# An MLP layer between scan layers: as a stage of its own, or in pieces beside the scan layers

## The chip, the cores and the metric

The kernel runs on one core of a Trainium2 chip, in one launch. The metric is device time in microseconds, the median of several executions. The core has five engines with a queue each: TensorE (PE), VectorE (DVE), ScalarE (ACT), GpSimd (POOL) and the sync engine (SP), which here only issues transfers. Each engine works through its own queue in order and waits on semaphores for the others.

## The reference

Eight images of 48 x 48 x 96, float32, go through four layers. Each layer is `x = x + layer(group_norm(x))`.

```python
x = x + _L0_conv_ref(_gn(x), ...)   # selective scan over the image in four directions
x = x + _L1_conv_ref(_gn(x), W1, b1, W2, b2, coef)
x = x + _L2_conv_ref(_gn(x), ...)   # four scans over rows and columns, restarted in each line
x = x + _L3_conv_ref(_gn(x), ...)   # as layer 0

def _L1_conv_ref(x, W1, b1, W2, b2, coef):
    xu = _upsample_rfft(xc)                          # to twice the size, band-limited
    h = h @ W1.T + b1                                # 96 -> 384
    h = coef[:, 0] + coef[:, 1] * h + coef[:, 2] * (h * h)
    h = h @ W2.T + b2                                # 384 -> 96
    out = _lpf_rfft(hc, cutoff=0.5)[:, :, ::2, ::2]  # low-pass, every second sample
```

Layers 0 and 3 are written once (`ss2d`), with their own weights. The images do not depend on each other.

## The kernel before

The four layers follow each other as four stages: `ss2d("l0")`, `spectral`, `lines`, `ss2d("l3")` (L1082 to L1085). Each opens its own pools of on-chip memory and closes them at its end, and hands its result on through HBM, one tensor an image (x1, x2, x3, L109).

**The scan layers.** `scans` (L188) lays out one long sequence by hand, and the order in which it calls engines is the order on their queues. There are 8 jobs (images) of 4 directions of 5 blocks of 10 or 8 rows: 160 blocks. A block has 8 slots (NG) in 4 turns, two slots a turn, a slot being some 4 us. In a turn ScalarE makes the decay factors `da` (L292, PSUM, two buffers) and copies a broadcast row `bc` to PSUM (`copy_b`, L249); VectorE and GpSimd share the inputs `dbu` (L268, four tiles, `rooms`); VectorE scans (L300); GpSimd multiplies by the output weights (`make_hc`, L306); TensorE sums over the states (`reduce`, L326 and L328), always for the turn before. The sync queue loads `bc` (L233) and `dd` (L221), which are sent to all partitions from a small copy in HBM that an earlier step stored (L446, L668).

**Work given out in slots.** At the end of each slot `aside(at)` (L370) issues what goes on the side: loads of the next block, one step of the generator `beside`, one step of stage 1 of a block two ahead (`run`), and the matmuls put in `tail`. In `ss2d` the generator `side` (L605) yields once per slot: the output work of the image before (`post`, L544), the group norm of the next image (`front`, L509), and its convolution (`conv`, L513). PSUM has eight banks: `da` takes four, `b` and `y` one each, and the two left are `s1` and `side` in `ss2d`, and `s1` with two buffers in `lines`.

**The MLP layer.** `spectral` (L893) uses that band-limiting is linear: the two image directions are enlarged and reduced by products with fixed matrices `upt` (48 x 73) and `downt` (73 x 48), and the square alone stays between. For each image: `heighten` (L921) enlarges one direction, and the result goes to HBM and back in another order; for 11 bands of 7 rows `widen` (L984) enlarges the other, `hidden` (L992) makes the 384 squares, `narrow` (L1001) brings them back to 96, `slim` (L1018) reduces one direction, and the result goes through HBM (`ydd`); `lower` (L959) reduces the other and adds the linear part, a product of x with a 96 x 96 matrix `wl` made from the norm (L951), the bias and x itself (L978, VectorE). `heighten` and `norm` of the next image and `lower` of the one before run beside the bands. Copies out of PSUM are shared between ScalarE and VectorE.

`lines` (L715) begins when `spectral` has closed its pools. Its `side` (L878) loads the next image after 8 slots and makes its norm later in the job.

Of the kernel before, what the change touches and what calls it, by code (L numbers as in the profile page):

```python
# [17 lines left out]
DH = 96  # L18
# [18 lines left out]
UR = 7  # L37
UCUT = (slice(0, 64), slice(64, UG))
NM = 3
# [58 lines left out]
def vss_stack_kernel(ctx: ExitStack, tc: tile.TileContext, i: dict, out: bass.AP):  # L98
# [41 lines left out]
    def group_norm(x, into, psum, behind=lambda step: step()):  # L140


        got = {}
        yield from norm_scale(x, got, psum, behind)
        for r0, nr in BLKS:
            nc.scalar.activation(into(r0, nr), x[:, r0:r0 + nr, :], AF.Identity, bias=got["shift"], scale=got["rs"])
            yield

    def norm_scale(x, got, psum, behind=lambda step: step()):
# [9 lines left out]
        for n in range(6):  # L159
            nc.vector.bn_stats(st[:, n, :], x[:, 8 * n:8 * n + 8, :])  # L160
            if n % 2:
                yield
        mv = small.tile([C, 2], F32, tag="mv", name="mv")
        nc.vector.bn_aggr(mv, st)
        yield
# [8 lines left out]
        for _ in range(7):  # L174
            yield
# [4 lines left out]
        yield  # L180
# [4 lines left out]
        yield  # L185


    def scans(dirs, order, restart, on_pool, a, pools, ps, stage1, opening, done, side, tail, ahead=None):  # L188
# [181 lines left out]
        def aside(at):  # L370

            nblk, slot = at // NG + 1, at % NG
            if nblk < len(blocks):
# [5 lines left out]
            next(beside, None)  # L379
# [3 lines left out]
            while tail:  # L383
                tail.pop(0)()

        for t, (b, q) in enumerate(turns):
# [29 lines left out]
            if q == NG // 2 - 1 and b.k == order[-1] and b.last:  # L416
                for _ in beside:
                    while tail:
                        tail.pop(0)()
        make_hc(nt - 1, 1)  # L420
# [50 lines left out]
    def ss2d(l, xin, xout, b0=0):  # L471
# [41 lines left out]
        def conv(b, blks, behind=lambda step: step()):  # L513
# [3 lines left out]
            for r0, nr in blks:  # L517
                n = nr * SEG
                for half in range(2):
                    pu = side_psum()  # L520
                    for slot in range(7):
                        for tap in ((0,), (1, 2), (3,), (4, 5), (6,), (7, 8), ())[slot]:
# [13 lines left out]
                        yield  # L536
# [4 lines left out]
                    yield  # L541
                    nc.sync.dma_start(zs[b][:, half, s], z[:, :n])

        def post(b, blks=BLKS):  # L544
# [4 lines left out]
            for r0, nr in blks:  # L549
# [8 lines left out]
                yield  # L558
                sq = lnp.tile([DH, 2, BMAX], F32, tag="sq", name="sq", bufs=1)
                nc.scalar.activation(sq[:, :, :n], yc, AF.Square)  # L560
                yield
# [7 lines left out]
                yield  # L569
            nc.scalar.activation(var[:, v0:v1], var[:, v0:v1], AF.Sqrt, bias=eps5[:CH])  # L570
            yield
            nc.vector.reciprocal(var[:, v0:v1], var[:, v0:v1])
            yield
            for r0, nr in blks:
                n = nr * SEG
                s = slice(r0 * W, r0 * W + n)
                z = lnp.tile([DH, LEAD + 2 * BMAX], F32, tag="zin", name="zin", bufs=1)
# [13 lines left out]
                yield  # L591
# [10 lines left out]
                yield  # L602
                nc.sync.dma_start(xout[b][:, s], xi[:, :n])

        def side(job):  # L605
# [9 lines left out]
            if job > 0:  # L615

                for _ in range(3):
                    used += 1
                    yield
                for _ in post(job - 1):  # L620
                    used += 1
                    yield
            if more:
                for _ in front(job + 1):
                    used += 1
                    yield

                while used < 10 * NG - 5:
                    used += 1
                    yield  # L630
                yield from conv(job + 1, BLKS, tail.append)
            else:

                for n, blk in enumerate(BLKS[:0:-1]):
                    while used < (NK * len(BLKS) - len(BLKS) + n + 1) * NG + 2:
                        used += 1
                        yield
                    for m, _ in enumerate(post(job, [blk])):
                        if m % 2:
                            used += 1  # L640
                            yield
# [61 lines left out]

        dirs, tail = DIRS_SS, []
# [4 lines left out]
        scans(dirs, (0, 1, 3, 2), False, ON_POOL_SS, a, pools, ps, stage1, opening, done, side, tail, conv(0, BLKS[1:3]))  # L709
        for _ in post(nb - 1, BLKS[:1]):  # L710
            pass
        stack.close()


    def lines(xin, xout):  # L715
# [8 lines left out]
        def load_x(b):  # L724
            xs[b] = xpool.tile([C, L], F32, tag="x", name="x")
# [16 lines left out]
        def front(b, behind=lambda step: step()):  # L742
            xp = xpads[b % 2]
            yield from group_norm(seq(xs[b], False), lambda r0, nr: shift(xp, 0, 0)[:C, r0:r0 + nr, :], lambda: ps("s1", 2),
# [22 lines left out]
        for k in range(NK):  # L767
            nc.vector.tensor_mul(taps[:, k], taps[:, k], wl["l2_inu"][:, k].unsqueeze(1).to_broadcast([DH, 4, 2 * DH]))
            for half in range(2):
                nc.scalar.activation(diag[:, k, half, :], wc["ident"], AF.Identity, scale=w["l2_d"][:, k, half:half + 1])  # L770

                p = ps("s1", 2)
# [3 lines left out]
        def stage1(b):  # L776
# [9 lines left out]
            def conv(half):  # L786
                def run():
                    got["u", half] = ps("s1", 2)
# [17 lines left out]
            def s3():  # L806
                got["p"] = ps("s1", 2)
# [8 lines left out]
            def s5():  # L816
                s4()
                for half in range(2):
                    got[half] = ps("s1", 2)
# [10 lines left out]
            def s7():  # L830
                for half in range(2):
                    got["z", half] = ps("s1", 2)
# [18 lines left out]
        def done(b, half, y):  # L851
# [8 lines left out]
            def project():  # L860
                got["o"] = ps("s1", 2)
# [16 lines left out]
        def side(job):  # L878
            if job + 1 < nb:
                for _ in range(NG):  # L880
                    yield
                load_x(job + 1)
# [6 lines left out]
        scans(dirs, range(NK), True, ON_POOL_L2, a, pools, ps, stage1, opening, done, side, tail)  # L889
# [3 lines left out]
    def spectral(xin, xout):  # L893
# [3 lines left out]
        stack = ExitStack()  # L897

        def pool(name, bufs, **kw):
            return stack.enter_context(tc.tile_pool(name=name, bufs=bufs, **kw))  # L900
        wt, xpool, xtp, xhp, upp, zp, row, pp, dr = (
# [277 lines left out]
```

## Time and profile before

| | us |
|---|---|
| median of 3 runs (18397.78 to 18404.0) | 18399.97 |
| span of the profiled execution | 18409.2 |
| first scan layer, from the first filling of its pipeline to its last VectorE work | 45 to 5585 |
| MLP layer, until the first memset of the lines layer | 5585 to 6913 |
| lines layer with its filling | 6913 to about 12650 |
| last scan layer | about 12650 to 18409 |

Busy over the whole span: TensorE 14747.1 us (80%), VectorE 16140.7 (88%), ScalarE 13666.8 (74%), GpSimd 15136.4 (82%). One 480-column float32 matmul is two records of the profile. A line of a waits view names who waited, for whom, and then the total in us, the number of times and the longest one. A line of a windows view gives a stretch of time, its length, the busy time and the number of instructions of each engine, the mean granted clock of TensorE as a share of full speed, the DMA engines' busy share, and GB/s.

### The profile page before, as it was taken

Reading aid. Unit: us, or ns where it says so; the run is one execution under the profiler, and the core shown is the slowest. Engines: PE = TensorE matmul, PEld = TensorE weight load, DVE = VectorE, ACT = ScalarE, POOL = GpSimd, SP = SyncE. Lnnn points to the kernel's source line nnn. Section 1 sums busy time; section 2 is a strip of 40 time slices with the busy share of each in tenths; the row PEclk is TensorE's granted clock in tenths of the full one; section 3 lists DMA queues with packets and bytes.
Section 4 is the critical chain, followed back from the end, with each engine's and each line's share of the span. In section 5 each row is a group of like instructions: output and inputs, shape, how many; then the busy total and the mean of one; then the engine's idle time right before and its main releaser. Section 6 shows DMA issues by size and latency. Waiting matters only on the chain.

```text
span 18409.2 us, 167554 instructions
## 1 busy us (share of the span) xinstructions
PE 14747.1 (80%) x53500; PEld 4297.8 (23%) x53500; DVE 16140.7 (88%) x10329; ACT 13666.8 (74%) x20348; POOL 15136.4 (82%) x7999
## 2 busy tenths in 40 slices
PE   7777777777777897888988988988777777777777
PEld 1211211211214562222222222222121221221221
DVE  7999999999992228999999999997899999999998
ACT  6877887887772227888788888886788778778776
POOL 7999999999990007888888888887899999999998
PEclk7877877777767787888888888888778778777776
DMA  4544545544443324444444444443454455455454
GB/s 143 175 171 171 172 172 172 174 174 167 172 168 52 50 43 148 158 150 152 156 149 156 150 155 156 148 155 125 164 178 171 169 173 173 170 175 173 166 174 144
DMA packets 768448, 2836.47 MB, mean 154 GB/s; under 512 B 235724, under 2 KB 298668, under 8 KB 640926
## 3 DMA queue, kind: packets, MB, share of 16 engines
q1 hardware_dynamic: 767558, 2825.75, 45.4%
q8 instruction: 418, 6.85, 0.2%
q14 instruction: 472, 3.87, 0.1%
HBM read 2377.32 MB, written 448.17 MB: 153 GB/s over the span
## 4 chain that ended last, share of the span: by engine, by line
POOL 27%; PE 20%; DVE 16%; issue 14%; ACT 14%; DMA 8%; SPq 1%; POOLq 0%; ACTq 0%; DVEq 0%
POOL dbu L306 18%; DVE dbu L300 10%; POOL dbu L268 6%; PE ps_s L792 5%; ACT ps_da L292 5%; DVE dbu L268 4%; DMA dd<-dds 3%; POOL dds L460 3%; PE ps_y L326 3%; ACT L292 2%; DMA dd<-dd 2%; PE ps_h L998 2%; PE ps_y L1011 2%; PE ps_s L864 1%; ACT L827 1%
## 5 line engine op out<-in xcount | busy, mean ns | idle before, releaser
L300 DVE TENSOR_TENSOR_SCAN dbu<-ps_da,dbu 128x968 f32<-128x968 f32 (+3 forms) x5760 | 11820.3, 2075 | 559.7 <-ACT ps_da L292 447.5
L306 POOL TENSOR_TENSOR dbu<-dbu,bc 128x1440 f32<-128x1440 f32 (+1 forms) x3840 | 10061.9, 2633 | 1615.3 <-DVE dbu L300 1540.9
L292 ACT ACTIVATE ps_da<-dd,w_l_a 128x484 f32<-128x484 f32 (+3 forms) x11520 | 7433.6, 649 | 2878.2 <-DVE dbu L300 2651.5
L326 PE MATMUL ps_y<-dbu,w_red 128*32 128x480 f32 (+1 forms) x23040 | 4838.4, 735 | 1955.6 <-POOL dbu L306 1935.4
L328 PE MATMUL ps_y<-dbu,w_red 128*32 128x480 f32 (+1 forms) x7680 | 4797.9, 735 | 0.0
L268 DVE TENSOR_TENSOR dbu<-dd,ps_b 128x962 f32<-128x962 f32 (+5 forms) x2880 | 3833.4, 1331 | 264.9 <-ACT ps_b L249 150.6
L268 POOL TENSOR_TENSOR dbu<-dd,bc 128x481 f32<-128x481 f32 (+5 forms) x2240 | 3910.5, 1760 | 22.6 <-DMA dd<-dd 19.5
L326 PEld LDWEIGHTS ps_y<-dbu,w_red 128*32 128x32 f32 x23040 | 748.5, 124 | 5975.6 <-POOL dbu L306 4242.9
L792 PE MATMUL ps_s<-xpad,w_l_cw 128*128 128x480 f32 (+1 forms) x2560 | 1758.5, 839 | 0.0
L249 ACT COPY ps_b<-bc 128x482 f32<-128x482 f32 (+3 forms) x2720 | 1450.5, 533 | 233.4 <-DVE dbu L268 191.4
L525 PE MATMUL ps_side<-xpad,w_l_cw 128*128 128x480 f32 (+1 forms) x2880 | 1526.5, 657 | 18.9 <-ACT u L538 14.2
L292 ACT ACT_TABLE_LOAD x986 | 1265.0, 1283 | 17.6
L734 POOL MEMSET xpad<- 128x2760 f32 x2 | 4.7, 2404 | 1333.9 <-DVE x L978 1333.9
L322 PE MATMUL ps_y<-ysum,w_ident 96*96 96x480 f32 (+1 forms) x960 | 762.9, 885 | 315.9 <-ACT ysum L701 315.3
L650 PE MATMUL ps_s<-bcl,dtw 6*96 6x480 f32 (+1 forms) x1280 | 871.7, 770 | 103.7 <-ACT dds L654 93.2
L660 PE MATMUL ps_s<-u,w_l_xp 96*38 96x480 f32 (+1 forms) x1280 | 832.3, 781 | 20.3 <-ACT z L540 20.3
L460 POOL TENSOR_TENSOR dds<-dds,u 96x960 f32<-96x960 f32 (+1 forms) x320 | 706.8, 2209 | 156.3 <-ACT dds L678 156.3
L525 PEld LDWEIGHTS ps_side<-xpad,w_l_cw 128*128 128x128 f32 x2880 | 559.8, 217 | 1032.4 <-issue 905.2
L792 PEld LDWEIGHTS ps_s<-xpad,w_l_cw 128*128 128x128 f32 x2560 | 521.2, 208 | 1084.6 <-issue 977.2
L328 PEld LDWEIGHTS ps_y<-dbu,w_red 128*32 128x32 f32 x7680 | 687.5, 124 | 0.0
L833 PE MATMUL ps_s<-xpad,w_l_inz 96*96 96x480 f32 (+1 forms) x640 | 506.3, 925 | 86.4 <-ACT dds L827 70.5
L654 ACT ACTIVATE dds<-ps_s,w_l_dtb 96x480 f32<-96x480 f32 (+1 forms) x640 | 404.7, 632 | 212.5 <-PE ps_s L650 94.7
(147 smaller groups left out, 11759.8 us busy)
## 6 DMA issues: line engine op xcount, KB each, us to landing
dd<-dd SPq DMA_DIRECT2D x512, 1452.0 KB
bc<-bcd SPq DMA_DIRECT2D x1536, 480.0 KB
dd<-dd SPq DMA_DIRECT2D x256, 1440.0 KB
dd<-dds SPq DMA_DIRECT2D x512, 363.0 KB
dd<-dd SPq DMA_DIRECT2D x128, 1164.0 KB
bc<-bcd SPq DMA_DIRECT2D x384, 384.0 KB
dd<-dds SPq DMA_DIRECT2D x256, 360.0 KB
dd<-dd SPq DMA_DIRECT2D x64, 1152.0 KB
```

Of the source, the lines that this page charges most:

```text
L249: nc.scalar.copy(bps[t][:, :bcs[t][0].shape[1]], bcs[t][0])
L268: engine.tensor_mul(o, du, by.unsqueeze(1).to_broadcast([P, hi - lo, by.shape[1]]))
L292: nc.scalar.activation(da[:, at:at + b.m], b.got[half][:, u % 3, 0, :], AF.Exp, scale=a[:, b.k, ci:ci + 1])
L300: nc.vector.tensor_tensor_scan(db, da, db, 0.0, ALU.mult, ALU.add)
L306: nc.gpsimd.tensor_mul(h, h, bcs.pop(2 * t + sub)[1].unsqueeze(1).to_broadcast([P, 3, n]))
L326: nc.tensor.matmul(y[32 * g:32 * g + 32, :n], lhsT=wc["red"][:, :32], rhs=hc[:, g, b.at], start=False, stop=(slot == 3))
L328: nc.tensor.matmul(y[DH:, :n], lhsT=wc["red"][:, 32:], rhs=hc[:, 2, b.at], start=(slot == 0), stop=(slot == 3))
L460: nc.gpsimd.tensor_mul(du, dt, u)
L525: nc.tensor.matmul(pu[:, :n], lhsT=flat[:, at:at + P], rhs=xpad[:, r0 + dy:r0 + dy + nr, dx:dx + W], start=(tap == 0), stop=(tap == 8))
L650: nc.tensor.matmul(got["p"][:DH, :n], lhsT=dtw[2 * NS:, b.k, half, :], rhs=b.bcl[2 * NS:, :n], start=True, stop=True)
L660: nc.tensor.matmul(got["p"][:NBC, :n], lhsT=w[f"{l}_xp"][:, b.k, half, :], rhs=u[:, half], start=(half == 0), stop=(half == 1))
L792: nc.tensor.matmul(got["u", half][:, :n], lhsT=flat[:, at:at + P], rhs=shifted(off), start=(tap == 0), stop=(tap == 3))
```

## The change

`spectral` is gone as a stage. A class `Guest` holds the MLP layer as a generator of small items, and `aside` gives them out at the end of each slot of the first scan layer and of the lines layer. An item is a transfer or a VectorE step ("do"), a pause of some slots ("wait"), or a piece with one PSUM bank ("psum"): its matmuls are issued in one slot and the copy out of PSUM, always on ScalarE, at the start of the next slot (`settle`). A credit limits the pieces: one a slot in the first scan layer, 0.42 in `lines`. Image b of the MLP layer can start when `post` has stored it (`avail`), and `lines` loads it when it is `made`.

The banks are those of the side work: in `ss2d`, `side` in slots in which the generator says that the bank is free (`yield True`), and `s1` in slots 2, 5 and 6; in `lines` the two buffers of `s1` become two named banks, `sa` and `sb`. So that `side` is free more often, `conv` issues its nine taps in slots 2 to 5 instead of 0 to 5.

The pieces are smaller: bands of 5 rows (15 an image), x transposed in four loads of 24 channels, the enlarged rows `xh` stored in four times two transfers in runs of 24 channels (96 bytes) instead of two of whole rows, `ydd` read back in 12 times two loads. x is loaded a second time for the last step. The residual is part of the matmul: the matrix is `wlin * rs + ident`, and the copy out of PSUM with the bias is the result. In `post`, `sq` and `zin` now share one buffer, and the descriptor memory for transfers (`dynamic_dma_scratch_size`) is set to 2048.

```diff
-UR = 7
+UR = 5
+HC = 24
+HS = 8
+ZW = 4
...
         def aside(at):
             nblk, slot = at // NG + 1, at % NG
+            if guest:
+                guest.settle()
...
-            next(beside, None)
+            clear = next(beside, True)
             run(at)
...
             while tail:
                 tail.pop(0)()
+            if guest:
+                guest.turn(slot, clear)
...
-                    pu = side_psum()
                     for slot in range(7):
-                        for tap in ((0,), (1, 2), (3,), (4, 5), (6,), (7, 8), ())[slot]:
+                        if slot == 2:
+                            pu = side_psum()
+                        for tap in ((), (), (0, 1), (2, 3), (4, 5), (6, 7, 8), ())[slot]:
...
-                        yield
+                        yield slot < 2
...
+            guest.banks = lambda slot, clear: (["side"] if clear else []) + (["s1"] if slot in (2, 5, 6) else [])
...
-                    got["u", half] = ps("s1", 2)
+                    got["u", half] = ps("sa" if half else "sb", 1)
...
-                got["o"] = ps("s1", 2)
+                got["o"] = ps("sa", 1)
...
+                while guest.made <= job + 1:
+                    for _ in range(NG):
+                        yield
                 load_x(job + 1)
...
+        guest.banks = lambda slot, clear: {0: ["sa"], 2: ["sb"], 3: ["sa"], 6: ["sb"]}.get(slot, [])
+        guest.rate = 0.42
...
+        def settle(self):
+            while self.pending:
+                self.pending.pop(0)()
+
+        def turn(self, slot, clear):
+            ready, self.soon = [f for n, f in self.soon if n <= 1], [(n - 1, f) for n, f in self.soon if n > 1]
+            for step in ready:
+                step()
+            self.credit = min(self.credit + self.rate, 2.0)
+            if self.wait:
+                self.wait -= 1
+                return
+            banks = self.banks(slot, clear)
+            while True:
+                self.item = self.item or next(self.work)
+                kind, *of = self.item
...
+                if kind == "do":
+                    self.item = None
+                    of[0]()
+                    continue
+                if not banks or self.credit < 1.0:
+                    return
+                self.item = None
+                self.credit -= 1.0
+                self.put(self.psum(banks.pop(0)), *of)
...
+                    nc.vector.scalar_tensor_tensor(wl, wlin, rs, wc["ident"], ALU.mult, ALU.add)
...
+                def load_xt(c0):
+                    nc.sync.dma_start(xt, self.xin[b].rearrange("c (h w) -> h c w", w=W)[:, c0:c0 + HC, :])
...
+                for c0 in range(0, C, HC):
+                    for s0 in range(0, HC, HS):
+                        yield heighten(s0)
+                    yield "wait", 1
+                    if c0 + HC < C:
+                        yield "do", lambda: load_xt(c0 + HC)
+                    yield "wait", 1
+
+                    def keep():
+                        for s in UCUT:
+                            nc.sync.dma_start(upd[s, :, c0:c0 + HC], xh[s])
+                    yield "do", keep
+                    yield "wait", 2
...
+                for n in range(last + 1):
+                    yield hidden(n, 0)
+                    if n:
+                        yield slim(n - 1)
+                    yield hidden(n, 1)
+                    yield hidden(n, 2)
+                    if n < last:
+                        yield widen(n + 1)
+                    yield narrow(n, 0, 3)
+                    if bands[n][1] > 3:
+                        yield narrow(n, 3, UR)
...
+                def lower(n):
+                    v = xv[:, n * ZW:(n + 1) * ZW, :]
+
+                    def run(p):
+                        nc.tensor.matmul(p[:C, :ZW * H], lhsT=wl, rhs=v, start=True, stop=False)
+                        for j in range(ZW):
+                            nc.tensor.matmul(p[:C, j * H:(j + 1) * H], lhsT=zs[n % 2][:, j, :], rhs=downt,
+                                             start=False, stop=(j == ZW - 1))
+                        self.soon.append((1, lambda: load_z(n + 2)))
+                    return "psum", run, lambda p: nc.scalar.activation(v, rows(p[:C], ZW * H), AF.Identity, bias=bl)
...
     ss2d("l0", i["x"], x1, guest)
-    spectral(x1, x2)
-    lines(x2, x3)
+    lines(x2, x3, guest)
     ss2d("l3", x3, out)
...
+                   dynamic_dma_scratch_size=2048)
```

The pieces of the other steps (`widen`, `hidden`, `narrow`, `slim`) have the matmuls of the old functions with the new band height.

## The prediction

> **What bounds the kernel now.** I read the busy shares over time first, then each stage's sums, then windows within one image's cycle of the first scan layer, then single waits and a few microseconds of single queues. Over time (a digit is a tenth of busy, a slice 460 us):
>
> ```profile
> DVE  7999999999992228999999999997899999999998
> ACT  6877887887772227888788888886788778778776
> POOL 7999999999990007888888888887899999999998
> ```
>
> Three slices near the first third have VectorE and ScalarE at 2 and GpSimd at 0: that is the MLP layer (L893 on), in which only TensorE works. By stage, from the windows view (first scan layer, MLP layer, lines layer):
>
> ```profile
> core 0: us, PE busy (x) PEld busy (x) DVE busy (x) ACT busy (x) POOL busy (x), PEclk, DMA share, GB/s
> 45.00:5584.95 5539.95, 4223.76 (x15382) 1084.33 (x15380) 5224.86 (x3183) 4316.33 (x6518) 5089.48 (x2856) 0.76 0.49 169
> 5584.95:6913.26 1328.31, 1154.55 (x6604) 757.32 (x6604) 274.10 (x465) 278.69 (x481) 0.00 (x0) 0.78 0.35 49
> 6913.26:12650.00 5736.74, 4953.88 (x15627) 1317.54 (x15628) 5255.66 (x3377) 4622.94 (x6637) 4793.94 (x2196) 0.83 0.42 153
> ```
>
> The scan layers are held by VectorE (94% and 92%), with GpSimd close in the first (92%). ScalarE has 1224 and 1114 us free there, TensorE 1316 and 783. The MLP layer needs 1155 us of TensorE, 553 of ScalarE and VectorE together. So the question is what ScalarE and TensorE can take without making VectorE wait. The first scan layer answers it by itself, since one image's cycle (680 us) has two halves: norm and output work of neighbours (first five windows) and then the convolution of the next image (L525), which loads both engines more. Two windows of each half:
>
> ```profile
> 836.00:904.00 68.00, 53.48 (x212) 17.94 (x204) 66.86 (x42) 50.78 (x78) 62.35 (x32) 0.68 0.47 162
> 1040.00:1108.00 68.00, 44.76 (x154) 7.43 (x146) 65.98 (x43) 50.83 (x77) 59.65 (x33) 0.58 0.40 140
> 1176.00:1244.00 68.00, 52.93 (x196) 13.13 (x188) 66.95 (x38) 59.27 (x87) 65.52 (x34) 0.94 0.51 175
> 1312.00:1380.00 68.00, 52.56 (x202) 13.92 (x200) 64.29 (x37) 57.99 (x88) 63.15 (x38) 0.87 0.56 194
> ```
>
> Columns as above. In the convolution half ScalarE has 58 to 59 us of 68 (85 to 87%) against 51 (75%), and yet each such window holds 25 scans where the other half holds 23 to 25. TensorE does some 50 more matmul records and is hardly busier, because the granted clock is 0.87 to 0.94 there against 0.58 to 0.68.
>
> Waits of VectorE in the whole first scan layer (us in total, times, longest):
>
> ```profile
> DVE dbu L300 <- ACT ps_da L292: 103.9, 135, 3.4
> DVE dbu L268 <- ACT ps_b L249: 74.5, 2, 73.9
> DVE xi L601 <- PE ps_side L598: 51.1, 19, 6.8
> ```
>
> The second is the filling of the pipeline; the first is what a busier ScalarE would raise: 0.77 us each time.
>
> **Removed.** From the last VectorE work of the first scan layer to GpSimd's first memset of the lines layer nothing but the MLP layer runs (POOL L734 waits 1333.9 us for DVE L978). 6913.26 - 5584.95 = **-1328.3**. The filling of the lines layer behind it (6913 to 6979) stays: its tiles take the memory of the closed layer, as before.
>
> **Added, VectorE.** Per image (rows of the first scan layer): 6 bn_stats by 0.536 = 3.2, aggregate 0.3, L171 1.37, L172 2.66, L173 0.16, L181 0.14, L183 0.37, and the new 96x96 scalar_tensor_tensor about 0.26 (as L1044): 8.3 us. By 8: **+66**, all on the bound. Every PSUM copy that VectorE made goes to ScalarE.
>
> **Added, ScalarE and TensorE.** In the built program's queues an image has 132 evacuations on ScalarE. By rows: xh 12 by 0.78 (L934's 0.97 for 480 columns, cut to 384), xu and hq 60 by 0.50 (L999, 0.688 for 511, cut to 365), ym 29 by 0.31 to 0.39 (L1014), yd 15 by 0.55, last step 12 by 0.45, plus two table loads of 1.28: 67 us. TensorE: 1154.55/8 = 144 us. The queue order puts 5.34 images beside the first scan layer (from its second image on) and 2.66 beside lines, the last stored after 543 of 640 loads of dd while lines fetches it at 564, so `while guest.made` never holds the lines layer up.
> First scan layer: 5.34 x 67 = 358 us of ScalarE over 132 blocks of 34 us, 6 to 8 items a block in the light half, 3 in the convolution half. The light half then stands at 75 + 10 = 85%, where the convolution half stands now without loss; the latter goes from 86 to 90%. I take one more 0.77 us wait in every second block: **+51**. Below it 0; above it all 358.
> Lines: 2.66 x 67 = 178 us over 112 blocks. Waits of VectorE on ScalarE are 281 by 0.82 us now; one more per two blocks is 46. TensorE, at 86%, gets 2.66 x 144 = 383 us over 112 x 35.9 = 4020, so 95%; VectorE waits 142 us on it now (L855, L872, L870), and half as much again over 112 of 160 blocks is 50. **+96**. Bounds 0 and 383 (TensorE wholly exposed). The two named banks, sa and sb, are part of this: a convolution or projection queued behind a guest evacuation waits for ScalarE, and behind it on TensorE stand the reductions, which have four dbu rooms (17 us) of cover.
> In a sentence beside this: the Trainium skill, "TensorE: Matmul & The Clock Gate", section "What's actually happening", has the gate open to full after about 3.4 us of sustained work. The windows above go that way, but twenty records of L930 back to back took 15.6 us at 0.50, so the trace agrees in part only; by the rule alone the 50 us would be nil.
>
> **Moved, the transfers.** All go through the one sync queue, in order, past dd (L221) and bc (L233). Per image 69 transfers instead of 19; at 0.4 us of issue that is 160 us more over 11 ms of a queue that mostly waits, nothing. The load_xt, up and z pieces are 240 to 1152 packets, 1 to 5 us. The store of xh is new in kind: it was 73 whole rows, it becomes 4 x 3504 runs of 96 bytes. The nearest row is the z load, 3504 runs of 384 bytes. In the timeline of the sync queue, start and length first:
>
> ```profile
> 6101.14 16.64 SPq L966 DMA_DIRECT2D z<-ydd  x2
> ```
>
> and in windows of 3 us under it, DMA share and GB/s at the end:
>
> ```profile
> 6106.00:6109.00 3.00, 0.00 (x0) 0.00 (x0) 0.00 (x0) 0.00 (x0) 0.00 (x0) 0.50 1.49 91
> 6109.00:6112.00 3.00, 0.00 (x0) 0.00 (x0) 0.00 (x0) 0.00 (x0) 0.00 (x0) 0.50 1.49 96
> ```
>
> At some 93 GB/s, 1314 KB take about 15 us, in which the queue itself stands. In the built order 10 of 24 such stores beside the first scan layer come right between the second dd load and the bc pair, 3 more just ahead of that dd load. How early is that pair? In the timelines of the sync queue and of ScalarE:
>
> ```profile
> 2030.38 6.94 SPq L233 DMA_DIRECT2D bc<-bcd  x2
> ```
>
> ```profile
> 2044.56 0.55 ACT L249 COPY ps_b<-bc 128x482 f32<-128x482 f32 x1
> ```
>
> 14 us ahead of its reader, of which its own way takes 3 or so. So 15 - 11 = 4 us late each time, and what is late is ScalarE's copy, with all da behind it and VectorE's scan behind these. I take it for each, since those elsewhere stand ahead of other dd or bc loads: 32 stores x 4 = **+128**; bounds 0 and 32 x 15 = 480. By the Trainium skill, "DMA: Bandwidth & Descriptors", section "Specifications", runs under 512 bytes are read-modify-written; it speaks against this edit, gives no price here, and no run shows it yet.
>
> **Costed at nothing.** Convolution taps bunched in slots 2 to 5 (both ss2d layers): same matmuls, covered by TensorE's idle fifth; uncovered, 2 us late at the reductions, which have 17. One buffer for sq and zin: the first zin load follows the last reader of sq by four steps; uncovered, the sync queue would stand a slot (4 us) once an image. The smaller descriptor scratch: every transfer of the page is issued on SPq.
>
> **Sum.** -1328.3 + 66 + 51 + 96 + 128 = -987. On the profiled execution's 18409.2: 17422. That execution is 9.2 above the median of the runs, 18399.97, so the forecast is **17,410**, with 17,280 to 17,600 as its own range.
>
> **Rivals.**
> (1) All hidden: the added matmuls raise the clock as in the convolution windows and ScalarE stays ahead. Only VectorE's 66 remain: 18400 - 1328 + 66 = 17,138. For it: no loss between the two halves. Against: the convolution half gets 3 items on top of its 86%.
> (2) The 96-byte stores stall at full price: 480 instead of 128: 17,765. For it: the queue standing 16.64 us; against: 14 us of lead and stores not always ahead of the pair.
> (3) ScalarE and TensorE exposed: 358 and 383 in place of 51 and 96: 18,007. For it: in-order queues, VectorE already waits on both in lines; against: the two halves.
> (4) Slower than before: every one of 1058 evacuations reaches ScalarE before its matmul is done, since it follows it by one slot only, and da waits behind. It decides from (1328 - 66)/1058 = 1.19 us each. The nearest row, L654, also one slot behind its matmul, waited for TensorE 38 times of 272, 0.92 us each; with that at every evacuation 0.51 + 0.92 = 1.43, by 1058 = 1513: 18,651. Against: 38 of 272.
> That the change doesn't do what it says would be a lines layer waiting for images; the order of the queues excludes it.
>
> **Chances.** The predicted time is the forecast's, the likeliest. Forecast 0.57, (1) 0.17, (2) 0.12, (3) 0.10, (4) 0.04. The range takes in (1) and (2), 17,130 to 17,800, and leaves (3) and (4) out. 0.2% (37 us) is about what a measurement tells from no change: faster 0.95, same 0.01, slower 0.04.
>
> **What would show it.** No stretch with GpSimd at 0 between the scan layers; the first scan layer's 5540 at 5600 to 5750 us, the 5737 of lines at 5800 to 5900, the last layer unchanged within 20; VectorE's waits on L292 up by 50 to 120; waits on DMA for bc or dd up by 100 or more, just behind stores of upd. It is wrong if the last layer changes, if waits on DMA do not rise, or if ScalarE's waits on TensorE exceed 300 us.

## The result and the profile after

| | before | after |
|---|---|---|
| median of the runs, us | 18401.99 (18397.78 to 18404.58) | 17895.1 (17876.22 to 17905.77) |
| span of the profiled execution | 18409.2 | 17891.2 |

The ratio is 0.9722, with a 95% interval of 0.9708 to 0.9736: faster by 2.8%. The forecast was 17,410, its range 17,130 to 17,800; the time lies above both. 1328 us were taken out and 518 came off the span.

In the busy view over 40 slices of the changed kernel, no slice has GpSimd at 0 any more:

```profile
DVE  7998999898888788787888889996999999999998
ACT  6877878878787677787777778786878778778776
POOL 7988888888888677787777778886999999999998
```

The ends of the stages are read from GpSimd's rows of the tile `xpad`, which give, behind the three durations in ns, the first and the last start of its two memsets. Lines begins at the first number of L755, the last layer at the last number of L490 (its second memset is that of the last layer):

```profile
L490 POOL MEMSET xpad<- x2: 2182/2184/2187, 0.9 to 12324.4; 128x2500 f32 x2
L755 POOL MEMSET xpad<- x2: 2403/2406/2409, 5996.0 to 5998.3; 128x2760 f32 x2
```

In the kernel before, the second memset of the last layer starts at 12,816.7, after the last work of lines (VectorE's last addition to x starts at 12,816.6). So lines ends there, 167 us later than the "about 12650" from which the 5737 us of lines was taken; only the boundary moves. Read so in every run (the first layer before is 6913.3 less the MLP layer's 1328):

| stage, us | before | forecast | after |
|---|---|---|---|
| first scan layer | 5585 | 5776 (44 + 51 + 96 more) | 5996 |
| MLP layer | 1328 | 0 | 0 |
| lines | 5903 | 6053 (22 + 96 + 32 more) | 6328 |
| last scan layer | 5593 | 5593 | 5567 |

So the first layer is 220 us and lines 275 us above forecast, the last layer 26 below. VectorE's waits in the changed kernel, first scan layer (one line) and lines (three), and then the scan's line of the kernel before, in lines:

```profile
DVE dbu L304 <- ACT ps_da L296: 343.1, 273, 4.8
```

```profile
DVE dbu L304 <- ACT ps_da L296: 331.8, 337, 3.3
DVE gated L876 <- PE ps_y L332: 238.0, 127, 5.8
DVE x L893 <- PE ps_sa L885: 179.1, 75, 4.5
```

```profile
DVE dbu L300 <- ACT ps_da L292: 237.2, 287, 3.3
```

L304 is the scan (L300 before). Its waits for the decay factors were 104 us in the first layer and 237 in lines; those of the gate and of the addition to x for TensorE were 86 and 42 in lines. Waits for transfers did not move: GpSimd's for `bc` are 61 us (70 before), VectorE's for `dd` 84 (84 before).

What ScalarE itself waits for shows where the lateness starts. First scan layer, then lines, the lines of the waits view that name a piece:

```profile
ACT g_room L1109 <- PE ps_side L1107: 67.9, 54, 6.9
ACT g_room L1165 <- PE ps_side L1162: 55.2, 22, 6.0
ACT g_room L1119 <- PE ps_side L1117: 55.0, 34, 4.2
```

```profile
ACT g_room L1109 <- PE ps_sb L1107: 77.0, 53, 3.0
ACT g_room L1119 <- PE ps_sb L1117: 68.0, 36, 4.0
```

L1109, L1119 and L1165 are the copies out of PSUM of `hidden`, `narrow` and `lower`. Summed over all such lines ScalarE stands 758 us (454 of 1050 pieces) until a piece's matmul is done. The other way round, TensorE stands 600 us until a piece's copy is done, 500 of them in matmuls of the layers themselves, which need nothing of the piece but its bank:

```profile
PE ps_sa L854 <- ACT g_room L1109: 72.8, 37, 2.8
PE ps_s L665 <- ACT g_room L1109: 42.7, 20, 3.1
```

One such case in the timeline of lines (start, length, engine, line; in brackets the idle time before it and who ended it):

```profile
7999.58 1.85 PE L885 MATMUL ps_sa<-gated,wo 96*96 96x480 f32 x4
7999.82 0.54 ACT L253 COPY ps_b<-bc 128x480 f32<-128x480 f32 x1
...
8001.27 1.65 PE L1117 MATMUL ps_sb<-g_w2q,g_room 128*73 128x96 f32 x18
...
8002.96 0.40 ACT L1119 COPY g_room<-ps_sb 73x288 f32<-73x288 f32 x1 [2.59 <-PE ps_sb L1117]
...
8003.25 2.64 ACT L296 ACTIVATE ps_da<-dd,w_l_a 128x480 f32<-128x480 f32 x4
...
8003.40 7.74 PE L813 MATMUL ps_sb<-xpad,w_l_cw 128*128 128x480 f32 x8 [0.48 <-ACT g_room L1119]
```

TensorE is still with the projection (L885) when ScalarE, at 8000.36, has nothing left ahead of the copy L1119. It stands 2.59 us; the decay factors (L296) stand behind the copy. And the layer's own convolution on bank `sb` (L813) stands behind the copy too. This tie of two in-order queues, in both directions, is what the experiments were made for.

### The profile page after: what moved, and what is told of

It is laid out like the page before. It is cut to its first block, busy times and chain, and to the rows that moved or that the text cites. A ratio compares the mean times of both kernels' runs of the same rounds, so it can differ in the third digit from the quotient of the medians.

```text
span 17891.2 us, 168509 instructions
## 1 busy us (share of the span) xinstructions
PE 14657.1 (82%) x53740; PEld 4413.6 (25%) x53740; DVE 15977.6 (89%) x9976; ACT 13880.5 (78%) x20932; POOL 15155.4 (85%) x7999
## 5 line engine op out<-in xcount | busy, mean ns | idle before, releaser
L304 DVE TENSOR_TENSOR_SCAN dbu<-ps_da,dbu 128x968 f32<-128x968 f32 (+3 forms) x5760 | 11823.5, 2074 | 923.6 <-ACT ps_da L296 757.6
L296 ACT ACTIVATE ps_da<-dd,w_l_a 128x484 f32<-128x484 f32 (+3 forms) x11520 | 7424.3, 649 | 2511.4 <-DVE dbu L304 2282.1
L330 PE MATMUL ps_y<-dbu,w_red 128*32 128x480 f32 (+1 forms) x23040 | 4741.8, 731 | 1238.5 <-POOL dbu L310 1225.2
L332 PE MATMUL ps_y<-dbu,w_red 128*32 128x480 f32 (+1 forms) x7680 | 4705.9, 731 | 0.0
L330 PEld LDWEIGHTS ps_y<-dbu,w_red 128*32 128x32 f32 x23040 | 797.7, 126 | 5072.2 <-POOL dbu L310 2976.6
L536 PE MATMUL ps_side<-xpad,w_l_cw 128*128 128x480 f32 (+1 forms) x2880 | 1466.0, 651 | 42.1 <-ACT g_room L1109 12.7
L665 PE MATMUL ps_s<-bcl,dtw 6*96 6x480 f32 (+1 forms) x1280 | 952.0, 835 | 290.6 <-ACT dds L669 133.5
L813 PE MATMUL ps_sb<-xpad,w_l_cw 128*128 128x480 f32 (+1 forms) x1280 | 879.0, 839 | 90.4 <-ACT g_room L1109 33.7
L813 PE MATMUL ps_sa<-xpad,w_l_cw 128*128 128x480 f32 (+1 forms) x1280 | 864.6, 826 | 0.1
L332 PEld LDWEIGHTS ps_y<-dbu,w_red 128*32 128x32 f32 x7680 | 730.8, 126 | 0.0
L716 ACT COPY ysum<-ps_y 96x480 f32<-96x480 f32 (+1 forms) x640 | 472.0, 738 | 62.9 <-PE ps_y L332 61.5
L830 PE MATMUL ps_sa<-ub,w_l_xp 96*38 96x480 f32 (+1 forms) x640 | 344.3, 669 | 205.1 <-ACT ub L820 205.1
```

Of the source, the lines that this page charges most:

```text
L296: nc.scalar.activation(da[:, at:at + b.m], b.got[half][:, u % 3, 0, :], AF.Exp, scale=a[:, b.k, ci:ci + 1])
L304: nc.vector.tensor_tensor_scan(db, da, db, 0.0, ALU.mult, ALU.add)
L330: nc.tensor.matmul(y[32 * g:32 * g + 32, :n], lhsT=wc["red"][:, :32], rhs=hc[:, g, b.at], start=False, stop=(slot == 3))
L332: nc.tensor.matmul(y[DH:, :n], lhsT=wc["red"][:, 32:], rhs=hc[:, 2, b.at], start=(slot == 0), stop=(slot == 3))
L536: nc.tensor.matmul(pu[:, :n], lhsT=flat[:, at:at + P], rhs=xpad[:, r0 + dy:r0 + dy + nr, dx:dx + W], start=(tap == 0), stop=(tap == 8))
L665: nc.tensor.matmul(got["p"][:DH, :n], lhsT=dtw[2 * NS:, b.k, half, :], rhs=b.bcl[2 * NS:, :n], start=True, stop=True)
```

## The experiments

The whole is a median. The stages are read as above, from the one profiled execution, whose time lies up to 23 us from the median. Three runs (after, `e13_lines036`, `e14_lines236`) have the same code in the first layer and took 5996, 5974 and 5978 us there, so differences of a stage under some 20 us are not read.

| run | whole | first layer | lines | last layer |
|---|---|---|---|---|
| after | 17895 | 5996 | 6328 | 5567 |
| e1_moved | 18358 | 6886 with the MLP layer | 5894 | 5570 |
| e2_pe_only | 17360 | 5742 | 6047 | 5572 |
| e3_act_only | 17266 | 5733 | 5960 | 5570 |
| e4_no_dma | 17839 | 5975 | 6308 | 5574 |
| e5_aside_first | 19172 | 6270 | 7239 | 5671 |
| e6_uncoupled | 17467 | 5831 | 6094 | 5563 |
| e7_finish_last | 18911 | 6104 | 7192 | 5615 |
| e8_even_free | 17493 | 5834 | 6083 | 5567 |
| e9_odd_free | 17867 | 5975 | 6315 | 5574 |
| e10_da_first | 18090 | 6155 | 6358 | 5582 |
| e11_early6 | 18124 | 6220 | 6332 | 5575 |
| e12_bank_only | 17455 | 5761 | 6124 | 5567 |
| e13_lines036 | 17887 | 5974 | 6332 | 5571 |
| e14_lines236 | 17826 | 5978 | 6261 | 5567 |

### The rearrangement alone: e1_moved

```diff
-                        for tap in ((0,), (1, 2), (3,), (4, 5), (6,), (7, 8), ())[slot]:
+                        for tap in ((), (), (0, 1), (2, 3), (4, 5), (6, 7, 8), ())[slot]:
...
-                got["p"] = ps("s1", 2)
+                got["p"] = ps("sa", 1)
```

> The kernel before, with only the two rearrangements of the change that do not need the pieces: the convolution's taps bunched into four slots in both scan layers, and the lines layer's three own results put on the two named banks sa and sb in place of a ring of two under one name. The MLP layer stays a stage of its own. Stages of the kernel before: first scan layer 5585 us, lines 5903, last layer 5593. If the rearrangement itself is what costs the changed kernel (425 us more in lines), lines is above 6000 here. If it costs nothing, as I predicted, lines is 5870 to 5940 and the whole is 18,330 to 18,420; the last layer, which gained 26 us in the changed kernel and has nothing but the bunched taps and one shared buffer to gain it by, should then gain 15 to 30 us here too.

Ratio to before 0.9974 (0.9964 to 0.9985). Lines is at 5894, the last layer gains 22 us, as it did in the changed kernel (in the table, every run whose last layer keeps the order of the turn has 5563 to 5575 there; the kernel before has 5593), and the first copy of `xh` on VectorE in the MLP layer starts 17 us earlier (5588.0, before 5604.8). The rearrangement is no loss; the bunched taps are a small gain.

### Each load alone: e2_pe_only, e3_act_only

```diff
-                    return "psum", run, lambda p: nc.scalar.copy(ym[:, j0 * C:j1 * C], p[:UG, :(j1 - j0) * C])
+                    return "psum", run, None
```

That is the edit of e2_pe_only at `narrow`; the other five likewise. In e3_act_only the matmuls go and the copies read `w1` or `room`:

```diff
-                    return "psum", run, lambda p: nc.scalar.copy(ym[:, j0 * C:j1 * C], p[:UG, :(j1 - j0) * C])
+                    return "psum", lambda p: None, lambda p: nc.scalar.copy(ym[:, j0 * C:j1 * C], w1[:UG, :(j1 - j0) * C])
```

> The changed kernel without ScalarE's six large evacuations of the MLP's results (heighten, widen, hidden, narrow, slim, lower); matmuls, banks' turns and transfers stay, the MLP's result is not computed. Changed kernel: first scan layer 5996 us, lines 6328. Theory 1 (ScalarE's in-order queue stands at an evacuation whose matmul is late, and what is behind it, da for VectorE, is late with it) and theory 4 (the evacuations' own seconds on ScalarE, some 536 us in all, fill it): first layer 5600 to 5720, lines 5930 to 6080, whole 17,170 to 17,400. Theory 2 (TensorE's extra matmuls make the layers' own results late): first layer above 5850, lines above 6200, whole above 17,650. Theory 3 (transfers): as theory 2.

> The changed kernel without the MLP's large matmuls; the six evacuations stay, of the same sizes, and read a tile of SBUF that is there already, so that none of them can wait for TensorE. The MLP's result is not computed. Theory 1 (the stand at a late matmul): most of the loss goes, first layer 5640 to 5780, lines 5960 to 6120, whole 17,250 to 17,470. Theory 4 (the evacuations' own time): loss stays, first layer above 5880, lines above 6220, whole above 17,700. Theory 2 (TensorE's time): first layer under 5700, lines under 6050. Theory 3 (transfers): as theory 4.

17,360 and 17,266; the first layer of e2_pe_only, 5742, is a little above the 5720 that theories 1 and 4 allowed. Neither TensorE's added time nor ScalarE's makes the loss by itself. Over the kernel before, the first layer rises by 157 and 148 us, lines by 144 and 57 (both hold VectorE's and the transfers' share); in the changed kernel by 411 and 425, which is more than the two together.

### Transfers: e4_no_dma

```diff
                         for s in UCUT:
-                            nc.sync.dma_start(upd[s, :, c0:c0 + HC], xh[s])
+                            pass
```

> The changed kernel without the MLP's inner transfers (the transposed picture in, the store and load of the heightened picture, the store and load of the narrowed one); it computes on zeros. Theory 3 (transfers, 128 us in my sum, up to 480): whole 17,420 to 17,790, with VectorE's and POOL's waits for dd and bc down. Theories 1, 2 and 4: whole within 50 us of the changed kernel (17,850 to 17,950), first layer 5950 to 6020, lines 6280 to 6350.

17,839 (17,826 to 17,859): 57 us below the changed kernel, a little beyond the 50 that the other theories allowed. So leaving out all inner transfers is worth that much in this kernel, and the 128 us for the stores alone were too much.

### Both loads, untied: e6_uncoupled

```diff
-                    return "psum", run, lambda p: nc.scalar.copy(ym[:, j0 * C:j1 * C], p[:UG, :(j1 - j0) * C])
+                    return "psum", run, lambda p: nc.scalar.copy(ym[:, j0 * C:j1 * C], w1[:UG, :(j1 - j0) * C])
```

> The changed kernel with every matmul and every evacuation of the pieces in its place, but the six large evacuations read SBUF in place of the bank, so that none waits for its matmul and no bank waits for its evacuation. The MLP's result is not computed. With matmuls alone the first layer rose by 157 us over the kernel before and lines by 142; with evacuations alone by 148 and 55. If the loss of the changed kernel (411 and 425) is the waiting of one engine for the other, it is here at most the sum of the two: first layer 5700 to 5900, lines 6020 to 6110, whole 17,300 to 17,580. If it is the two engines' load taken together, whichever waits for which, the stages stay: first layer above 5950, lines above 6270, whole above 17,800.

17,467: with all matmuls and all copies in their places, 428 us are gone as soon as neither waits for the other at the bank, 165 in the first layer and 234 in lines (the profiled execution of this run is 22 us above its median). ScalarE's waits at pieces fall from 758 to 62 us, TensorE's for their copies from 600 to 9; what is left are waits over tiles in SBUF. So the tie is most of the loss. The granted clock doesn't order these runs: 0.777 in the changed kernel, 0.784 here, 0.756 in e3_act_only, the fastest. VectorE's wait for the decay factors over the whole run falls from 757.6 us to:

```profile
DVE dbu L304 <- ACT ps_da L296: 549.2, 580, 7.3
```

### The place in the turn: e5_aside_first, e7_finish_last, e8_even_free, e9_odd_free

```diff
-            if t > 0:
-                reduce(t - 1, 1)
             aside(at)
+            if t > 0:
+                reduce(t - 1, 1)
```

> The changed kernel with two statements of a turn exchanged: the slot's side work (first matmuls of the next block, and the pieces) is given out ahead of the second reduction of the turn before, not behind it, so that on TensorE's queue a piece's matmul no longer stands behind a reduction that waits for GpSimd's product. Everything computed is the same. Theory 1a (pieces' matmuls are late because they stand behind that reduction): ScalarE's waits for TensorE at the pieces' evacuations, 758 us in the changed kernel, fall below 400, first layer below 5850, lines below 6200, whole 17,480 to 17,750. Theory 1b (they are late because the banks are handed from piece to layer and back, whatever stands ahead): waits stay above 600, whole within 80 us of 17,895. A third way: the reductions are now late behind the pieces, ends of y and the gate (VectorE's line 876) wait longer, whole above 17,950.

Ratio to before 1.0415 (1.0399 to 1.043): 1277 us slower than the changed kernel. TensorE's waits and the wait of VectorE's gate in this run:

```profile
PE ps_sa L830 <- ACT ub L820: 741.6, 160, 5.5
PE ps_s L665 <- ACT dds L669: 652.7, 242, 9.8
```

```profile
DVE gated L876 <- PE ps_y L332: 1390.3, 276, 13.8
```

The exchange moved not only the pieces ahead of the reduction but the layer's own matmuls of the slot, and these wait for ScalarE within the slot (L830 after the activation L820; 205 us of waits in the changed kernel). The reduction stands behind them, and y is late. So the run came out as the third way, by matmuls that I had not counted, and did not decide on theory 1a. It shows that the reduction has its place for a reason.

```diff
-            finish(at + 1)
             aside(at + 1)
+            finish(at + 1)
```

> The exchange of the run before (side work ahead of the second reduction), and besides the end of an output block (its copy on ScalarE in the first layer, its product with the gate on VectorE in lines) given out behind the odd slot's side work, not ahead of it. If the exchange alone makes ScalarE and VectorE wait at that end, this takes it back: 20 to 80 us less than the exchange alone, VectorE's wait at line 876 under 150 us. If nothing waits there, it is within 30 us of the exchange alone; if the later end holds up the next opening of y, it is slower than that by 30 us or more.

18,911, 261 us better than the exchange alone, but not where expected: the copy of y on ScalarE (L716) waits 304 us in place of 753, the gate (L876) still 1340.

Untying by slot asks the same question without moving anything. `self.cut` is set when a piece is given out:

```diff
+                self.cut = slot % 2 == 0
                 self.put(self.psum(banks.pop(0)), *of)
...
-                    return "psum", run, lambda p: nc.scalar.copy(ym[:, j0 * C:j1 * C], p[:UG, :(j1 - j0) * C])
+                    return "psum", run, lambda p: nc.scalar.copy(ym[:, j0 * C:j1 * C], self.src(p, w1)[:UG, :(j1 - j0) * C])
```

> The changed kernel, with the large evacuations of the pieces given out on even slots reading SBUF in place of their bank; pieces of odd slots stay tied to theirs. The MLP's result is not computed. A count of the pieces by slot: 416 even and 292 odd ones in the first layer, 307 even and 35 odd ones in lines, so 69% are even. With all of them untied the kernel took 17,467 us, 428 less than the changed kernel. An even slot's matmul goes out right behind the second reduction of the turn before, which waits for GpSimd, and only a pair of da and a copy of b lie between it and its evacuation on ScalarE; an odd slot's goes out with nothing waiting ahead of it and two pairs of da before its evacuation. If that place is what makes the stand (theory 1a, in spite of the exchange that failed), untying the even ones takes back 360 us or more: whole 17,460 to 17,530. If every piece costs alike (theory 1b), it takes back 69%, some 295 us: whole 17,560 to 17,640.

> The same with the pieces of odd slots untied and those of even slots tied. Theory 1a: takes back 70 us at most, whole 17,820 to 17,900. Theory 1b: takes back some 130 us, whole 17,730 to 17,800, nearly all of it in the first layer, where 292 of the 327 odd pieces are.

17,493 and 17,867: 402 us for the 69% of pieces on even slots, 28 for the others. With the odd ones alone tied (e8_even_free), ScalarE still stands 230 us for pieces' matmuls, and that costs next to nothing; TensorE's waits for pieces' copies are down to 23 us. With the even ones alone tied (e9_odd_free), ScalarE stands 531 us and TensorE 596, nearly as in the changed kernel. So the banks that come back late are those of even pieces, and the price goes by the place in the turn. Why an even place is dear, by the matmul that starts late, by what stands behind the copy, or by the bank, these two do not tell.

### Later and earlier copies: e10_da_first, e11_early6

```diff
-            make_da(t, 1)
             make_dbu(at + 2, nc.gpsimd)
...
             finish(at + 1)
+            make_da(t + 1, 1)
             aside(at + 1)
```

> The changed kernel with one call moved in every turn of all three layers: the second pair of da of the next turn is given to ScalarE ahead of the odd slot's side work, not behind the next turn's first scan. So an even slot's evacuation comes one pair of da (1.36 us in the trace) later on ScalarE, and its matmul has that time more. Everything computed is the same. If the stand at even pieces costs by ScalarE's queue (402 of 428 us were theirs), the stand of 1 to 1.5 us is mostly covered: ScalarE's 758 us of waits at evacuations under 350, whole 17,550 to 17,750. If instead the bank's late return to TensorE is what costs, the later evacuation makes it worse: TensorE's waits for evacuations rise, whole 17,950 to 18,300. The last layer, which has no pieces, tells what the move does by itself: I expect 5540 to 5620 there (5567 in the changed kernel).

18,090, 195 us worse: ScalarE's waits at pieces fall only from 758 to 695 us, TensorE's for pieces' copies rise from 600 to 878. ScalarE's waits for VectorE at the decay factors rise too, from 2282 to 2484, and the copies now stand behind these as well: they come later by more than the 1.36 us that was meant. The last layer, which has no pieces, is at 5582, so the move by itself costs little. In this order a later copy buys less on one queue than it costs on the other.

```diff
+            if guest:
+                guest.early(at % NG)
             if t > 0:
                 reduce(t - 1, 1)
             aside(at)
```

> The changed kernel with one kind of piece given out earlier on TensorE's queue: in the first layer, the piece on bank s1 at slot 6 (77 of the 416 even ones) goes out ahead of the turn's second reduction, everything else of that slot stays behind it. Unlike the exchange of all side work, no matmul that waits for ScalarE is moved ahead of the reduction. Even pieces cost 162 us for 416 in the first layer, 0.39 us each. If the place behind the reduction makes the cost, these 77 give back 20 to 40 us: first layer 5950 to 5980; if not, it stays at 5985 to 6005. Lines and the last layer as in the changed kernel.

The edit did more than its expectation says: `aside` begins with `settle`, so the 77 pieces' copies also went out a slot earlier, right behind the reduction. The first layer went to 6220. It is no test of theory 1a, but the nearest to a price for ScalarE's stand at an even piece: its waits at pieces rose by 195 us (758 to 953), TensorE's for their copies did not (600 to 585), and the whole lost 229 us. What the 77 pieces' matmuls cost by going ahead of the reduction is in that too, and was not separated.

### Half of the tie: e12_bank_only

Against e3_act_only:

```diff
-                    return "psum", lambda p: None, lambda p: nc.scalar.copy(ym[:, j0 * C:j1 * C], w1[:UG, :(j1 - j0) * C])
+                    return "psum", lambda p: None, lambda p: nc.scalar.copy(p[:UG, :(j1 - j0) * C], w1[:UG, :(j1 - j0) * C])
```

> The evacuations alone, as in the run without the MLP's large matmuls (17,266 us; first layer 5733, lines 5958), but each writes its values into its bank in place of SBUF, so that the layer's next matmul on that bank waits until ScalarE is through with it, while ScalarE itself waits for no matmul. The MLP's result is not computed. This is one half of the tie, the bank's return, without the other, ScalarE's stand. If the bank's return makes the loss: first layer above 5850, lines above 6100, whole above 17,500. If ScalarE's stand makes it: first layer 5720 to 5780, lines 5940 to 6010, whole 17,250 to 17,370.

17,455: neither forecast fits the whole. The first layer takes 27 us more than in e3_act_only, near what two runs of the same code differ by; lines takes 164 more. The copies differ in more than their target: written into the bank they take ScalarE 507 us in place of 615 (those of `xh` 0.47 us each in place of 1.16), so both prices may be too low. In lines the return of the bank shows in TensorE's wait for the copy (here into `ps_sa`) and in VectorE's addition behind it (36.8 us in e3_act_only):

```profile
PE ps_sa L854 <- ACT ps_sa L1105: 128.9, 36, 5.5
```

```profile
DVE x L893 <- PE ps_sa L885: 189.2, 86, 4.2
```

In the first layer TensorE waits 500 us for these copies, and it costs little. L854 is the gate's matmul at slot 1, on the bank that a piece took at slot 0; the projection L885 stands behind it on TensorE. So the two layers seem to differ: in lines a good part of the tie is the bank, in the first layer little of it. There ScalarE's stand remains, by elimination; no run isolated it with the matmuls in their places.

### Which slots: e13_lines036, e14_lines236

```diff
-        guest.banks = lambda slot, clear: {0: ["sa"], 2: ["sb"], 3: ["sa"], 6: ["sb"]}.get(slot, [])
+        guest.banks = lambda slot, clear: {2: ["sb"], 3: ["sa"], 6: ["sb"]}.get(slot, [])
```

> The changed kernel, in lines alone with the pieces' slots cut from 0, 2, 3 and 6 to 0, 3 and 6; everything computed is the same. By count 228 even and 114 odd pieces in lines in place of 307 and 35, the same 342 in all, spread over more blocks. An even piece's tie cost 248 us for 307 there, 0.81 us each, an odd one's next to nothing. If the cost goes by the even pieces, 79 fewer of them give back 64 us: lines 6250 to 6290, whole 17,810 to 17,860. If it goes by the number of pieces, or slot 2 is not dear but slot 0 and 6 are, lines stays at 6310 to 6345.

> The same with slots 2, 3 and 6: 232 even and 110 odd pieces in lines. By the even pieces 61 us back, lines 6250 to 6290, whole 17,810 to 17,860, as with slots 0, 3 and 6. If one even slot is dearer than the other, the two runs differ: at slot 0 the layer needs the bank in the next slot for its gate, and TensorE's waits there (line 854) were the longest of its waits for evacuations in lines, so leaving slot 0 out should be the better by 10 to 40 us.

Without slot 2: 17,887, lines 6332, nothing gained. TensorE's waits for copies fell by 83 us (L813, 83 to 1) and it did not matter. Without slot 0: 17,826, lines 6261, 68 less. The price goes by the slot, not by the number of even pieces. Ratio to before 0.969 (0.9676 to 0.9703), against 0.9722 (0.9708 to 0.9736) of the changed kernel: this version beats both kernels. Its waits in lines, VectorE's and then ScalarE's, and last ScalarE's for VectorE in lines of the changed kernel:

```profile
DVE gated L876 <- PE ps_y L332: 338.5, 135, 5.8
DVE dbu L304 <- ACT ps_da L296: 331.1, 341, 3.3
...
DVE x L893 <- PE ps_sa L885: 33.8, 46, 1.9
```

```profile
ACT ps_da L296 <- DVE dbu L304: 500.9, 482, 7.3
ACT g_room L1109 <- PE ps_sa L1107: 171.9, 40, 6.2
```

```profile
ACT ps_da L296 <- DVE dbu L304: 741.2, 646, 7.3
```

The addition to x waits 34 us in place of 179, and L854 waits for no piece any more (164 before); the gate waits 101 us more and takes part of it back. ScalarE stands longer for pieces than in the changed kernel, 603 us in place of 398 in lines, since the 110 pieces at slot 3 are late by 4.2 us on average. But its wait for VectorE at the decay factors fell by more, from 741 to 501, and the scan's wait for them is unchanged (332 and 331). A stand where ScalarE would have waited for VectorE anyway costs nothing; that is how I read these rows, no run isolates it.

## Why the prediction was wrong

- **Removed, -1328.3.** Right: the stage is gone, and GpSimd with it never idle for a slice.
- **Added, VectorE, +66.** The rows of the pieces add up to 84.4 us (112 instructions); 18 too few, nearly all in two steps of an image: 1.37 and 1.20 us where I had 0.37 and 0.26 (L1052, L1053).
- **Added, ScalarE and TensorE, +51 and +96: the step that failed.** It priced a load: so much more ScalarE, one more wait of 0.77 us in every second block. The loads were a tenth and a fifth larger than said (ScalarE's pieces 593 us with the small ones, my 8 x 67 = 536; TensorE's 1383, my 1155). What was left out is that a piece binds TensorE's queue to ScalarE's twice within one slot. Untying the two queues took off 428 us, against the 485 by which the median missed. That the untied kernel, at 17,467, falls into the forecast's own range is partly luck: its first layer and lines rose by 437 us, and less VectorE's 84 and at most 57 for transfers that leaves some 300 (an estimate) for the two loads, where I had 51 + 96 = 147. The 128 us for transfers, too many, hid it. The half sentence on banks `sa` and `sb` named one direction of the tie and gave it no term of its own; rival (4) named the other.
- **Rival (4)** had the mechanism, and its row (38 of 272, 0.92 us) was used to dismiss it. 454 of 1050 copies found their matmul unfinished, by 1.67 us each on average, 0.72 over all. With the copies' own 0.56 us that is 1.29 for each piece, above the 1.19 from which it expected a loss, and the kernel still gained 2.8%: so its price, all of ScalarE's added time exposed, was wrong as well. The row L654 was no guide for the pieces; those at even slots have their matmul behind the reduction and the layer's own, but that this is why they are dear was not shown. Nor would waits by count have given the price: 230 us of them, the odd ones, cost 28.
- **Rival (3)**, 18,007, is nearest in number, for another reason: it took the added load to be exposed, and e2_pe_only and e3_act_only show each load mostly hidden.
- **Transfers, +128.** Too much: without any inner transfer the kernel is 57 us faster. The sync queue stood 6.5 us in the median for each of the 32 stores of `xh` (two issues each) and 12.9 at most, not the 15 that I took from the z load of as many runs of 384 bytes; all but two of the 32 were within the 11 us that I had counted as covered. The Trainium skill, "DMA: Bandwidth & Descriptors", section "Specifications", has runs under 512 bytes read-modify-written; here 96-byte runs cost the kernel less than I had feared, and no run isolates that rule.
- **Costed at nothing.** The bunched taps gave 22 us in the last layer (e1_moved), where I had "unchanged within 20"; the sign was in the kernel's favour. The shared buffer was not tried alone.
- **What would show it.** All three signs named for a wrong forecast came: the last layer changed (by 26 us), waits for transfers did not rise, and ScalarE's waits on TensorE went over 300 us. Only the last one points at the step that failed.

What stays open: why an even place is dear; how the 234 us of the tie in lines divide between the bank (164 by e12_bank_only, but without the pieces' matmuls; 68 by leaving slot 0 out) and ScalarE's stand, and which even slots are dear in the first layer.

## What to carry to other kernels

When small pieces of work are slipped into an in-order schedule, cost the tie and not the load: what stands ahead of the piece's matmul on TensorE, what stands behind its copy on ScalarE, and who needs the bank next. A kernel that does all the work but reads other data in the copies measures that tie in one run. Waits do not add up to a price: in e14_lines236 ScalarE's stands grew by 204 us and lines became 68 us shorter, while its waits for VectorE fell by 240.

## What the runs showed of the hardware

Most copies of the pieces took within 0.15 us of what their nearest rows before had let me expect. The copy of `xh` did not: 1.13 us for 73 x 384 where the row for 480 columns, 0.98, had let me expect 0.78. The same copy took 1.16 us from SBUF (e3_act_only) and 0.47 written into a PSUM bank in plain order (e12_bank_only), so reading PSUM is not what makes it long; whether the target or the order of writing does, no run tells. In the transfers the surprise went the other way: the stores of `xh` are four times as many and in 96-byte runs, and the waits for `dd` and `bc` stayed at 84 and 61 us where they had been 84 and 70.
